# Keys of a cross-attention left unnormalized, and their last tiles shared between batches

## The chip, the core and the metric

The kernel runs on one core of a Trainium2 chip. The core has five engines that work side by side, each through its own instructions in order: TensorE (PE in the profile; its weight loads are PEld), VectorE (DVE), ScalarE (ACT), GpSimd (POOL), and SyncE (SP), which here issues all DMA transfers. Engines wait for each other through semaphores. The metric is device time in microseconds (us) of one execution; lower is better. Time before: median 2002.96 us of three runs (2000.17 to 2003.44).

## What is computed

One block of a Perceiver: x has 8 batches of 64 tokens with 512 features, the context 8 batches of 1601 tokens. A cross- and self-attention block, a sparse self-attention and a feed-forward network are added to x in turn. The part that matters here is the cross attention, with 8 groups of keys (128 features each) and two heads per group:

```python
kvx = jnp.einsum('bsi,oi->bso', cond, w_kv_x)
kx, vx = jnp.split(kvx, 2, axis=-1)
kx = _ln(kx.reshape(b, sc, g, d), kxln_w, kxln_b)
vx = vx.reshape(b, sc, g, d)
xout = _gqa(qx, kx, vx).reshape(b, s, nh * d)
```

`_ln` takes the mean off, multiplies by `rsqrt(var + 1e-5)`, then by a weight and adds a bias, both along the features. `_gqa` is softmax of q k / sqrt(128) over the 1601 tokens, times v.

## The kernel before

The cross attention is done in 16 pieces of work (class `Cross`): two halves of four key groups, and in each half the 8 batches. A batch's 1601 tokens are 13 tiles (`TT`), twelve of 128 tokens and a last one of 65; its tiles form six chunks (`CHUNKS`), five of two tiles and a last one of three, 321 tokens. So there are 208 steps (variable `g` in the main loop at L1142), with one tile of keys each; other work is laid between them.

Per tile, `keys` (L529) loads the transposed context (`cTr`), splits it into a high and a low part (`cThi` by ACT, `cTlo` by POOL), and multiplies both with the key weights, high and low, in 12 matmuls (L542) whose moving side is 512 columns, the four groups' features. [...] `key_weights` (L491) has taken the mean out of the weights, so that keys come out centred. ACT squares (`sq`, L547) and copies (`kn`, L548) the result; DVE sums the squares by group (`kxv`, L549), POOL adds epsilon and raises to -1/2 (`rqk`, L550 and L173), and DVE multiplies the keys by it (L552). One step later `keys_t` (L555) transposes the tile on PE (L219), ACT writes weight times key plus bias as the high part (`kthi`, L565), DVE subtracts it (`kf`, L567), and ACT adds the bias and writes the low part (`ktlo`, L568).

When a chunk is complete, `scores` (L570) multiplies the queries, high and low, with the keys of each group (L587), three matmuls a group, into banks of PSUM. DVE copies each group's scores to SBUF (`S`) while it takes their maximum (`cmx`, L591); the second operand of that instruction is a column of zeros. For the last chunk the odd 321st column is padded to 322 with zeros by POOL (L576, L577). `maxima` (L594) reduces the chunks' maxima, and `exps` (L598) takes the exponentials with the negative maximum as ACT's bias. 16 steps after a tile's keys, `probs_t` (L604) transposes its probabilities, `context` (L636) loads the context, and `weigh` (L661) multiplies them (L676 to L678). `values` and `cat` follow at the end of a batch.

Between the steps the loop pumps streams of other work (projections, self attention, output projections, the conversion of the feed-forward weights) at fixed paces; `pin` and `paced` name an instruction after which the pumped work may be issued. Within each engine the order is set when the program is built, by a scheduler that simulates time; on the chip each engine takes its instructions in that order.

PSUM tiles come from three pools: `pm` (tag m, 3 banks: keys, scores, transposed probabilities), `pb` (one), and `pacc` (4, the sums of `weigh`). `kf` has two buffers of 2 KB per partition, also used by `key_weights` at the start (L495) and by the last attention (`pd`, L155).

Of the kernel before, what the change touches and what calls it, by code (L numbers as in the profile page):

```python
# [11 lines left out]
F32 = mybir.dt.float32  # L12
F32R = mybir.dt.float32r
# [8 lines left out]
P = 128  # L22
# [13 lines left out]
CHUNKS = [(0, 1), (2, 3), (4, 5), (6, 7), (8, 9), (10, 11, 12)]  # L36
KTW = 324
NCH = len(CHUNKS)
CHUNK_OF = {tt: ci for ci, ch in enumerate(CHUNKS) for tt in ch}
LAG = 17  # L40
ALL = 10 ** 6
# [4 lines left out]
PACE = 1.55, 4  # L46
LATER = 142
TERNARY_PACE, TERNARY_AT = 0.4, 8
HELD = "held"


# [6 lines left out]
def tile_perceiver(ctx: ExitStack, tc: tile.TileContext, t: dict):  # L58
# [18 lines left out]
    def nm(s):  # L77
        uid[0] += 1
        return f"{s}_{uid[0]}"
# [62 lines left out]
    class Late:  # L142
# [9 lines left out]
        fb = _main("cThi", 2)  # L152
        ld = _main("qxlo", 1)
        xrt = _main("qxhi", 1)
        pd = _main("kf", 2)  # L155
        ps = staticmethod(lambda tag="b": kxp())

        AT = {"hT": (0, 0), "ps_": (0, 0), "qkv": (0, 256), "sim": (0, 448), "mask": (1, 0), "eq": (1, 64), "cum": (1, 128),
# [332 lines left out]
    def key_weights(half):  # L491
        hi = mp.tile([P, NIC, 512], F32R, tag="wkhi", name=nm("wkhi"), bufs=1)
        lo = mp.tile([P, NIC, 512], F32R, tag="wklo", name=nm("wklo"), bufs=1)
        for ic in range(NIC):
            tag, bufs = ("kf", 2) if half == 0 and ic >= 2 else ("raw", 3)  # L495
            raw = load(mp.tile([P, 512], F32, tag=tag, name=nm("wkr"), bufs=bufs), t["wkv"][ic * P:(ic + 1) * P, half * 512:(half + 1) * 512])
            raw3 = v3(raw, HG)
            mu = sm("wkmu", HG)
            V.tensor_reduce(mu, raw3, AX.X, ALU.add)
            V.scalar_tensor_tensor(raw3, mu.unsqueeze(2).to_broadcast([P, HG, D]), -1.0 / D, raw3, ALU.mult, ALU.add)  # L500
            A.copy(hi[:, ic, :], raw)
            (V if half else GP).tensor_tensor(lo[:, ic, :], raw, hi[:, ic, :].bitcast(F32), ALU.subtract)
        return hi, lo

    paced = [None]
    pin = [None]

    class Cross:


        def __init__(self, b, half):
            self.b, self.half = b, half
            self.raw = None
            self.S = {}
            self.kt = {}
            self.kn = {}
            self.pp = {}
            self.cc = {}
            self.mx = sm("cmx", HG * NCH, bufs=2)
            self.su = sm("csu", HG * NCH, bufs=2)  # L520

# [7 lines left out]
        def keys(self, tt):  # L529

            t0, n = TT[tt]
            raw = mp.tile([P, NIC, P], F32, tag="raw", name=nm("cTr"), bufs=3)
            paced[0] = nc.sync.dma_start(raw[:, :, :n], t["ctxT"][self.b].rearrange("(c p) k -> p c k", p=P)[:, :, t0:t0 + n])
            chi = mp.tile([P, NIC, P], F32R, tag="cThi", name=nm("cThi"), bufs=2)
            clo = mp.tile([P, NIC, P], F32R, tag="cTlo", name=nm("cTlo"), bufs=2)
            A.copy(chi[:, :, :n], raw[:, :, :n])  # L536
            GP.tensor_tensor(clo[:, :, :n], raw[:, :, :n], chi[:, :, :n].bitcast(F32), ALU.subtract)  # L537
            ps = kxp()
            k = 0
            for st, mv in ((chi, self.wk[0]), (chi, self.wk[1]), (clo, self.wk[0])):  # L540
                for ic in range(NIC):
                    PE.matmul(ps[:n], lhsT=st[:, ic, :n], rhs=mv[:, ic, :], start=k == 0, stop=k == 11)  # L542
                    k += 1
            kn = mp.tile([P, 512], F32, tag="kn", name=nm("kn"), bufs=3)
            sq = mp.tile([P, 512], F32, tag="sq", name=nm("sq"), bufs=1)
            v = sm("kxv", HG)
            A.activation(sq[:n], ps[:n], AF.Square, scale=1.0 / math.sqrt(D))  # L547
            A.copy(kn[:n], ps[:n])  # L548
            V.tensor_reduce(v[:n], v3(sq[:n], HG), AX.X, ALU.add)  # L549
            GP.tensor_scalar(v[:n], v[:n], EPS, None, ALU.add)  # L550
            r = rsqrt(v[:n], n, HG, "rqk")
            pin[0] = V.tensor_tensor(v3(kn[:n], HG), v3(kn[:n], HG), r.unsqueeze(2).to_broadcast([n, HG, D]), ALU.mult)  # L552
            self.kn[tt] = kn

        def keys_t(self, tt):  # L555

            t0, n = TT[tt]
            ci = CHUNK_OF[tt]
            c0 = TT[CHUNKS[ci][0]][0]
            if ci not in self.kt:  # L560
                self.kt[ci] = [mp.tile([P, HG, KTW], F32R, tag="kt" + x, name=nm("kt" + x), bufs=2) for x in ("hi", "lo")]
            hi, lo = self.kt[ci]
            pt = transpose4(self.kn.pop(tt), n, kxp())
            o = slice(t0 - c0, t0 - c0 + n)
            A.activation(hi[:, :, o], v3(pt, HG)[:, :, :n], AF.Identity, bias=hb["kx"], scale=hw["kx"])  # L565
            kf = mp.tile([P, HG, P], F32, tag="kf", name=nm("kf"), bufs=2)
            V.scalar_tensor_tensor(kf[:, :, :n], v3(pt, HG)[:, :, :n], hw["kx"], hi[:, :, o].bitcast(F32), ALU.mult, ALU.subtract)  # L567
            A.activation(lo[:, :, o], kf[:, :, :n], AF.Identity, bias=hb["kx"])  # L568

        def scores(self, ci):  # L570
            chunk = CHUNKS[ci]
            cw = sum(TT[tt][1] for tt in chunk)
            hi, lo = self.kt.pop(ci)
            N = cw + (cw & 1)
            if N > cw:
                GP.memset(hi[:, :, cw:N].bitcast(F32), 0.0)  # L576
                GP.memset(lo[:, :, cw:N].bitcast(F32), 0.0)  # L577
            sc = mp.tile([P, HG, KTW], F32, tag="S", name=nm("S"), bufs=7)
            self.S[ci] = sc
            per = 512 // N  # L580
            for g0 in range(0, HG, per):
                bank = mainp("s")
                gs = range(g0, g0 + per)

                for k, (a, x) in enumerate(((self.qhi, hi), (self.qlo, hi), (self.qhi, lo))):
                    for i, g in enumerate(gs):
                        PE.matmul(bank[:, i * N:(i + 1) * N], lhsT=a[:, g * P:(g + 1) * P], rhs=x[:, g, :N],  # L587
                                  start=k == 0 and i == 0, stop=k == 2, skip_group_check=True)
                for i, g in enumerate(gs):
                    ps = bank[:, i * N:(i + 1) * N]  # L590
                    V.tensor_tensor_reduce(sc[:, g, :cw], ps[:, :cw], zeros.to_broadcast([P, cw]), 1.0, -3.0e38,  # L591
                                           ALU.add, ALU.max, self.mx[:, g * NCH + ci:g * NCH + ci + 1])

        def maxima(self):  # L594
            self.nmx = sm("cnm", HG)
            V.tensor_reduce(self.nmx, v3(self.mx, HG), AX.X, ALU.max, negate=True)  # L596

        def exps(self, ci, g0=0, g1=HG):  # L598
            cw = sum(TT[tt][1] for tt in CHUNKS[ci])
# [367 lines left out]
            xs.append((xr, j * P, i * P, P))  # L967
        return z, xs

    def gp_copy(dst, src):  # L970
        GP.tensor_scalar(dst, src, 1.0, 1.0, ALU.mult, ALU.mult)  # L971

    WIDEN = gp_copy, A.copy

    def ffn_weights(f, kind):
# [151 lines left out]
            token_norm(j)  # L1127
            yield

    NT = len(TT)  # L1130
    work = [Cross(b, half) for half in range(2) for b in range(NB)]
    NA = NT * len(work)
    rest = range(1, NJ)
# [8 lines left out]
    for g in range(NA + LAG + 3):  # L1142
# [24 lines left out]
            last_context()  # L1167
        if g < NA:
            work[nA].keys(kA)
        if g == 0:  # L1170
            bgA.pump(ALL)
        if g == 2:
            bgA.add(norms(rest), projection("qx", range(4), rest), projection("qx", range(4, 8), range(NJ)),
                    projection("q", range(8), range(NJ)), projection("k", range(4), range(NJ)), projection("v", range(4), range(NJ)))
# [134 lines left out]
```

## Time and profile before

| | us |
|---|---|
| median of the runs | 2002.96 |
| profiled execution, its own time | 1998.47 |
| span of its instructions | 1996.7 |
| PE busy | 1931.5 (97%) |
| PEld busy | 1594.1 (80%) |
| DVE busy | 1357.9 (68%) |
| ACT busy | 1345.9 (67%) |
| POOL busy | 682.7 (34%) |
| DMA engines, mean busy share | 55.8% |

The profile is of one execution. The span runs from the first to the last instruction; the execution's own time includes 1.8 us around it. In a row of instructions, "busy" is the time in which at least one of the group ran, followed by the mean length of one in nanoseconds, and then the idle time of the engine before them and what ended it. Matmuls overlap each other, so that their lengths add up to more than their busy time. The granted clock of TensorE was 0.987 on average.

### The profile page before, as it was taken

The page shows a single profiled execution, that of the slowest core. Times are in us where ns is not written, and L with a number is a line of the kernel's source. Part 1 is how long each engine was busy: PE and PEld are TensorE (multiplying, and loading weights), DVE is VectorE, ACT ScalarE, POOL GpSimd, SP SyncE. Part 2 cuts the span into 40 slices and gives each one's busy share as a digit, 9 for nine tenths or more (in the row PEclk, how much of TensorE's full clock was granted, in tenths as well). Part 3 has the DMA queues.
Part 4 walks back from the last instruction along what each step waited for, and adds up shares of the span by engine and source line. Part 5 has one row for each costly group of instructions (what it writes and reads, how often), then busy time and mean ns, then how long its engine had stood idle before and what let it go on. Part 6 is the DMA issues. An engine that isn't in the chain of part 4 may idle for free. (4 is left out here: it accounts for less than half of the span.)

```text
span 1996.7 us, 32526 instructions
## 1 busy us (share of the span) xinstructions
PE 1931.5 (97%) x10709; PEld 1594.1 (80%) x10709; DVE 1357.9 (68%) x3324; ACT 1345.9 (67%) x2932; POOL 682.7 (34%) x807
## 2 busy tenths in 40 slices
PE   6899999999999999999999999999999999999998
PEld 5688887888888888888888888888877777886776
DVE  6868678667778677766775765666577665665665
ACT  6777777677778667765765655665786676676554
POOL 5443434333334434323233323323333323320132
PEclk9999999999999999999999999999999999999989
DMA  6354445466455654556886667656744633564415
GB/s 195 112 151 148 148 146 153 132 193 213 152 150 172 194 179 140 173 180 224 282 268 192 214 225 264 203 185 214 258 133 154 212 110 97 165 205 139 149 56 172
DMA packets 296507, 352.05 MB, mean 176 GB/s; under 512 B 30337, under 2 KB 191233, under 8 KB 296337
## 3 DMA queue, kind: packets, MB, share of 16 engines
q1 hardware_dynamic: 296336, 349.97, 55.8%
q8 instruction: 84, 1.38, 0.3%
q14 instruction: 87, 0.70, 0.1%
HBM read 283.94 MB, written 65.68 MB: 175 GB/s over the span
## 5 line engine op out<-in xcount | busy, mean ns | idle before, releaser
L537 POOL TENSOR_TENSOR cTlo<-cTr,cThi 128x512 fp32r<-128x512 f32 (+1 forms) x208 | 271.1, 1303 | 840.7 <-PE kx L542 443.8
L677 PE MATMUL acc<-plo,chi 128*128 128x512 f32 x768 | 311.7, 406 | 1.0 <-DVE plo L624 1.0
L678 PE MATMUL acc<-phi,clo 128*128 128x512 f32 x768 | 303.4, 396 | 0.0
L549 DVE TENSOR_REDUCE kxv<-sq 128x4 f32<-128x512 f32 (+1 forms) x208 | 141.9, 682 | 228.0 <-ACT sq L547 227.7
L542 PE MATMUL kx<-wkhi,cThi 128*128 128x512 f32 (+1 forms) x832 | 244.3, 415 | 6.6 <-DVE cmx L591 2.5
L676 PE MATMUL acc<-phi,chi 128*128 128x512 f32 x768 | 237.8, 403 | 4.6 <-ACT chi L653 3.4
L565 ACT ACTIVATE kthi<-kx,cols 128x512 fp32r<-128x512 f32 (+1 forms) x208 | 159.5, 767 | 106.8 <-PE kx L219 105.1
L542 PE MATMUL kx<-wklo,cThi 128*128 128x512 f32 (+1 forms) x832 | 231.0, 398 | 0.0
L542 PE MATMUL kx<-wkhi,cTlo 128*128 128x512 f32 (+1 forms) x832 | 226.3, 393 | 0.0
L173 POOL TENSOR_TENSOR rqk<-kxv,mhalf 128x4 f32<-128x4 f32 (+1 forms) x208 | 219.9, 1057 | 16.6
L653 ACT CAST chi<-cr 128x512 fp32r<-128x512 f32 x192 | 118.9, 619 | 137.7 <-PE acc L677 126.2
L536 ACT CAST cThi<-cTr 128x512 fp32r<-128x512 f32 (+1 forms) x208 | 125.6, 605 | 120.0 <-PE kx L542 48.4
L601 ACT ACTIVATE S<-S,cnm 128x256 f32<-128x256 f32 (+1 forms) x384 | 196.8, 520 | 1.5 <-DVE cnm L596 1.5
L567 DVE SCALAR_TENSOR_TENSOR kf<-kx,cols,kthi 128x512 f32<-128x512 f32 (+1 forms) x208 | 151.1, 726 | 60.0 <-ACT kthi L565 58.8
L542 PEld LDWEIGHTS kx<-wklo,cThi 128*128 128x128 f32 (+1 forms) x832 | 156.2, 188 | 39.7
L542 PEld LDWEIGHTS kx<-wkhi,cTlo 128*128 128x128 f32 (+1 forms) x832 | 153.5, 185 | 39.3 <-issue 0.8
L552 DVE TENSOR_TENSOR kn<-kn,rqk 128x512 f32<-128x512 f32 (+1 forms) x208 | 144.7, 695 | 57.0 <-POOL rqk L173 55.5
L542 PEld LDWEIGHTS kx<-wkhi,cThi 128*128 128x128 f32 (+1 forms) x832 | 147.2, 189 | 40.8 <-DVE cmx L591 5.0
L591 DVE CUSTOM_DVE_ANT_0 S<-s,zeros 128x256 f32<-128x256 f32 (+1 forms) x384 | 149.7, 429 | 43.8 <-PE s L587 43.5
L568 ACT ACTIVATE ktlo<-kf,cols 128x512 fp32r<-128x512 f32 (+1 forms) x208 | 147.4, 709 | 29.0 <-DVE kf L567 28.5
L676 PEld LDWEIGHTS acc<-phi,chi 128*128 128x128 f32 x768 | 139.0, 189 | 34.9 <-ACT chi L653 4.6
L677 PEld LDWEIGHTS acc<-plo,chi 128*128 128x128 f32 x768 | 145.2, 189 | 25.7 <-DVE plo L624 1.5
(339 smaller groups left out, 3938.3 us busy)
## 6 DMA issues: line engine op xcount, KB each, us to landing
cTr<-in_ctxT SPq DMA_DIRECT2D x192, 256.0 KB
cr<-in_ctx SPq DMA_DIRECT2D x192, 256.0 KB
ws<-wpd SPq DMA_DIRECT2D x88, 512.0 KB
clod<-clo SPq DMA_DIRECT2D x96, 256.0 KB
clo<-clod SPq DMA_DIRECT2D x96, 256.0 KB
wv<-in_wkv SPq DMA_DIRECT2D x64, 256.0 KB
tern<-in_ffn_w SPq DMA_DIRECT2D x64, 256.0 KB
wpd<-ws SPq DMA_DIRECT2D x32, 512.0 KB
```

The costliest lines, as they stand in the source:

```text
L173: GP.tensor_tensor(y[:n], v, mhalf[:n, :k], ALU.pow)
L537: GP.tensor_tensor(clo[:, :, :n], raw[:, :, :n], chi[:, :, :n].bitcast(F32), ALU.subtract)
L542: PE.matmul(ps[:n], lhsT=st[:, ic, :n], rhs=mv[:, ic, :], start=k == 0, stop=k == 11)
L552: pin[0] = V.tensor_tensor(v3(kn[:n], HG), v3(kn[:n], HG), r.unsqueeze(2).to_broadcast([n, HG, D]), ALU.mult)
L565: A.activation(hi[:, :, o], v3(pt, HG)[:, :, :n], AF.Identity, bias=hb["kx"], scale=hw["kx"])
L567: V.scalar_tensor_tensor(kf[:, :, :n], v3(pt, HG)[:, :, :n], hw["kx"], hi[:, :, o].bitcast(F32), ALU.mult, ALU.subtract)
L568: A.activation(lo[:, :, o], kf[:, :, :n], AF.Identity, bias=hb["kx"])
L591: V.tensor_tensor_reduce(sc[:, g, :cw], ps[:, :cw], zeros.to_broadcast([P, cw]), 1.0, -3.0e38, ALU.add, ALU.max, self.mx[:, g * NCH + ci:g ...
L601: A.activation(self.S[ci][:, g, :cw], self.S[ci][:, g, :cw], AF.Exp, bias=self.nmx[:, g:g + 1], accum_out=self.su[:, g * NCH + ci:g * NCH ...
L676: PE.matmul(self.U[ic], lhsT=chi[:n, s], rhs=phi[:n], start=tt == 0, stop=False)
L677: PE.matmul(self.U[ic], lhsT=chi[:n, s], rhs=plo[:n], start=False, stop=False)
L678: PE.matmul(self.U[ic], lhsT=clo[:n, s], rhs=phi[:n], start=False, stop=False)
```

## The change

Four things change. First, keys are no longer multiplied by their norm, and the bias is left off: `turned` writes weight times raw key as high part (ACT) and low part (DVE). The norms `rqk` go to a buffer in DRAM (`rd`), and when a chunk's last tile is done, `spread` loads the chunk's norms back into all 128 partitions (`rb`, tokens by groups). The evictions of the scores multiply by `rb` where they read zeros before. The product of query and bias is the same for all tokens and falls out of the softmax; it is computed as one more column of keys, in place of the padding column of the last chunk, and copied out (`cqb`), and `maxima` adds it and takes it off again.

Second, the last 64 full tokens of two neighbouring batches share one tile of keys of 128, computed in the step of the even batch; the odd batch has no key matmuls in its last step. Batches 0 and 1 of the first half keep a last tile of 65 each. Third, the 1601st tokens of all 8 batches form one small tile per half (`odd_keys`, at steps 30 and 110), whose keys are stored beside the bias column and copied into place by ACT. Fourth, the scratch for software DMAs is declared smaller; `rb` takes the place of `kf` wherever that served.

```diff
+    def raw_keys(wk, chi, clo, n, held=False):
+        ps = kxp()
+        k = 0
+        for st, mv in ((chi, wk[0]), (chi, wk[1]), (clo, wk[0])):
+            for ic in range(NIC):
+                PE.matmul(ps[:n], lhsT=st[:, ic, :n], rhs=mv[:, ic, :], start=k == 0, stop=k == 11)
+                k += 1
+        kn = mp.tile([P, 512], F32, tag="kn2" if held else "kn", name=nm("kn"), bufs=1 if held else 3)
...
+        pin[0] = V.tensor_reduce(v[:n], v3(sq[:n], HG), AX.X, ALU.add)
+        GP.tensor_scalar(v[:n], v[:n], EPS, None, ALU.add)
+        r = rsqrt(v[:n], n, HG, "rqk")
+        return kn, r
+
+    def turned(kn, n, parts, r0=0):
+        hi, lo = parts
+        pt = kxp()
+        for g in range(HG):
+            PE.transpose(pt[:, g * P:g * P + n], kn[:, g * P:(g + 1) * P], ident[r0:r0 + n, r0:r0 + n])
+        src = v3(pt, HG)[:, :, :n]
+        A.activation(hi, src, AF.Copy, scale=hw["kx"])
+        V.scalar_tensor_tensor(lo, src, hw["kx"], hi.bitcast(F32), ALU.mult, ALU.subtract)
+
+    def odd_keys(half):
+        raw = load(mp.tile([P, 512], F32, tag="raw", name=nm("oc"), bufs=3)[:NB], t["ctx"][:, SC - 1, :])
+        pt = kxp()
+        for ic in range(NIC):
+            PE.transpose(pt[:, ic * NB:(ic + 1) * NB], raw[:, ic * P:(ic + 1) * P], ident[:NB, :NB])
...
+        kn, r = raw_keys(wk[half], chi, clo, NB)
+        oddr[half] = dtile([NB, HG], F32, f"oddr{half}")
+        nc.sync.dma_start(oddr[half], r)
...
+        turned(kn[:NB], NB, [x[:, :, :, 0] for x in oddk[half]])
...
         def keys(self, tt):
             t0, n = TT[tt]
+            pair = tt == NT - 1 and self.paired
+            if pair and self.b % 2:
+                return
...
-            A.activation(sq[:n], ps[:n], AF.Square, scale=1.0 / math.sqrt(D))
-            A.copy(kn[:n], ps[:n])
-            V.tensor_reduce(v[:n], v3(sq[:n], HG), AX.X, ALU.add)
-            GP.tensor_scalar(v[:n], v[:n], EPS, None, ALU.add)
-            r = rsqrt(v[:n], n, HG, "rqk")
-            pin[0] = V.tensor_tensor(v3(kn[:n], HG), v3(kn[:n], HG), r.unsqueeze(2).to_broadcast([n, HG, D]), ALU.mult)
+            kn, r = raw_keys(self.wk, chi, clo, n, pair)
             self.kn[tt] = kn
+            if pair:
+                nxt = work[self.half * NB + self.b + 1]
+                nxt.kn[tt] = kn
+                self.rt = nxt.rt = dram.tile([P, HG], F32, tag="rt", name=nm("rt"), bufs=2)
+                nc.sync.dma_start(self.rt, r)
+                return
...
+            nc.sync.dma_start(self.rd[ci][o:o + n], r)
+
+        def spread(self, ci):
+            cw = sum(TT[tt][1] for tt in CHUNKS[ci])
+            rb = self.rb[ci] = mp.tile([P, KTW, HG], F32, tag="rb", name=nm("rb"), bufs=RB)
...
+            for o, src in parts:
+                w = src.shape[0]
+                load(rb[:, o:o + w].rearrange("p t g -> p (t g)"), src.rearrange("t g -> (t g)").partition_broadcast(P))
...
-            A.activation(hi[:, :, o], v3(pt, HG)[:, :, :n], AF.Identity, bias=hb["kx"], scale=hw["kx"])
-            kf = mp.tile([P, HG, P], F32, tag="kf", name=nm("kf"), bufs=2)
-            V.scalar_tensor_tensor(kf[:, :, :n], v3(pt, HG)[:, :, :n], hw["kx"], hi[:, :, o].bitcast(F32), ALU.mult, ALU.subtract)
-            A.activation(lo[:, :, o], kf[:, :, :n], AF.Identity, bias=hb["kx"])
+            r = self.b % 2 * S
+            turned(kn[r:r + S], S, [x[:, :, o:o + S] for x in self.kt[ci]], r)
+            for x, y in zip(self.kt[ci], oddk[self.half]):
+                A.copy(x[:, :, o + S:o + S + 2], y[:, :, self.b, :])
...
-                    V.tensor_tensor_reduce(sc[:, g, :cw], ps[:, :cw], zeros.to_broadcast([P, cw]), 1.0, -3.0e38,
-                                           ALU.add, ALU.max, self.mx[:, g * NCH + ci:g * NCH + ci + 1])
+                    V.tensor_tensor_reduce(sc[:, g, :cw], ps[:, :cw], rb[:, :cw, g], 1.0, -3.0e38,
+                                           ALU.mult, ALU.max, self.mx[:, g * NCH + ci:g * NCH + ci + 1])
+                    if N > cw:
+                        V.tensor_copy(self.qb[:, g:g + 1], ps[:, cw:N])
 
         def maxima(self):
+            top = sm("ctop", HG)
+            V.tensor_reduce(top, v3(self.mx, HG), AX.X, ALU.max)
+            V.tensor_tensor(top, top, self.qb, ALU.add)
             self.nmx = sm("cnm", HG)
-            V.tensor_reduce(self.nmx, v3(self.mx, HG), AX.X, ALU.max, negate=True)
+            V.tensor_tensor(self.nmx, self.qb, top, ALU.subtract)
...
         if g < NA:
             work[nA].keys(kA)
+            if kA == CHUNKS[CHUNK_OF[kA]][-1]:
+                work[nA].spread(CHUNK_OF[kA])
...
+        if g in ODD_AT:
+            odd_keys(work[nA].half)
...
-    nc = _bacc.Bacc("TRN2", target_bir_lowering=False, num_devices=1)
+    nc = _bacc.Bacc("TRN2", target_bir_lowering=False, num_devices=1, dynamic_dma_scratch_size=1024)
```

Constants: `UNPAIRED = 2`, `ODD_AT = 30, 110`, `RB = 2` (buffers of `rb`, 5 KB per partition each). `self.paired` is true for all batches of the second half and for batches 2 to 7 of the first.

## The prediction

> **What bounds the kernel.** I read the page's totals first, then the stretches, then single instructions of TensorE. Columns of the first two rows: the share of each engine; of the stretches: length, then busy time and count of PE, PEld, DVE, ACT, POOL, the granted clock, DMA share, GB/s.
>
> ```profile
> span 1996.7 us, 32526 instructions
> PE 1931.5 (97%) x10709; PEld 1594.1 (80%) x10709; DVE 1357.9 (68%) x3324; ACT 1345.9 (67%) x2932; POOL 682.7 (34%) x807
> ...
> 0.00:100.00 100.00, 75.82 (x382) 61.57 (x383) 76.31 (x215) 71.43 (x149) 51.82 (x67) 0.94 0.51 154
> ...
> 1000.00:1400.00 400.00, 397.62 (x2203) 334.71 (x2202) 252.47 (x560) 244.33 (x525) 128.67 (x153) 1.00 0.68 222
> ...
> 1800.00:1996.70 196.70, 180.73 (x998) 133.59 (x994) 120.37 (x283) 106.64 (x206) 43.78 (x49) 0.94 0.43 130
> ```
>
> PE is full except in the first 100 us and, less, the last 200; no other engine passes 77% in any stretch. [...] So I look at starts, not at busy time (timeline of PE; start, length, instruction):
>
> ```profile
> 1782.81 1.10 PE L542 MATMUL kx<-wklo,cThi 128*65 128x512 f32 x4
> 1783.75 1.10 PE L542 MATMUL kx<-wkhi,cTlo 128*65 128x512 f32 x4
> 1784.69 0.60 PE L219 MATMUL kx<-ident,kn 128*128 128x128 f32 x4
> ...
> 1791.78 0.41 PE L219 MATMUL kx<-ident,kn 65*128 65x65 f32 x4
> 1792.03 0.60 PE L613 MATMUL pt<-ident,S 128*128 128x128 f32 x4
> ```
>
> Four matmuls of 512 columns start 0.94 us apart from the next four: one occupies PE for **0.235 us**, not the 0.4 us of its row, and the 65-row tile pays as much as a full one. Over the whole trace, start-to-start steps longer than is usual for the same pair of instructions add up to 143 us, some 83 of them between 200 and 1800 us. So PE is occupied about 93% of the span: nearer to the 97% than to the 80%. A PE instruction removed is time removed, at 0.235 us.
>
> **Part 1, tiles of keys (PE).** Before, 16 tiles of 65 tokens pay 12 matmuls each. After, batches 0 and 1 of the first half keep theirs (2), the other 14 share 7, and the odd tokens take 2 tiles: 11. The built order shows 2496 key matmuls becoming 2436. 60 x 0.235 = **14.1 us off**. Transposes: 64 of 65 columns become 8 of 65, 56 of 64, and 16 of 8 for the odd tokens; by the fence four small ones take 0.25 us, so 16 more cost **1.0 us**. Scores, probabilities and contexts keep every PE instruction. PE: **-13.1 us**, nearly all in the stretch that is full.
>
> **Part 2, the norm leaves the keys (DVE, ACT).**
>
> ```profile
> L552 DVE TENSOR_TENSOR kn<-kn,rqk 128x512 f32<-128x512 f32 x192 | 133.7, 696 | 51.0 <-POOL rqk L173 49.7
> ...
> L568 ACT ACTIVATE ktlo<-kf,cols 128x512 fp32r<-128x512 f32 x192 | 139.1, 724 | 26.9 <-DVE kf L567 26.6
> ...
> L885 DVE TENSOR_TENSOR ps__4142_16875<-pr x1: 357/357/357, 1548.6 to 1548.6; 128x192 f32<-128x192 f32 x1
> ...
> L888 DVE TENSOR_TENSOR ps__4142_16875<-ps__4142_16875,pmx x1: 347/347/347, 1550.7 to 1550.7; 128x192 f32<-128x192 f32 x1
> ...
> L897 DVE TENSOR_REDUCE ao<-pr x4: 811/836/855, 1555.8 to 1957.8; 128x64 f32<-128x384 f32 x3, 64x64 f32<-64x384 f32 x1
> ```
>
> All 208 multiplies by the norm go (page: 208 x 695 ns = 145 us of DVE), and all 208 second ACT passes over the low part (208 x 709 ns = 147 us). The low part is written by the DVE instruction that wrote kf (L567), so its count stays but for the tiles; five fewer reduces (L549) give 3.4 us.
>
> What comes in return is the read in the eviction of the scores (L591, 384 of them): it multiplies by rb[:, :, g], whose elements stand 16 bytes apart, where before it read one constant. The trace has no row of exactly this. [...] The rows agree in kind: 8-byte steps (L885) cost as much as contiguous ones (L888), 256-byte steps (L897) 836 ns for 384 elements and (L887) 505 for 192, so 1.72 ns an element, where the evictions themselves go from 418 ns at 256 to 486 at 321, or 1.05. Ends: 0 if the step is free, +0.68 ns an element if it costs what L897 pays. [...] With 64 copies of one column (164 ns by L817) and two more small operations per batch, 16 us: DVE 1358 - 145 - 3 + 70 + 16 = 1296 us (1226 at the other end); ACT 1346 - 147 - 6 for fewer tiles + 28 copies x 0.2 (L633) = 1199. POOL loses 32 memsets and five tiles' small operations, about 10 us. The two odd tiles bring some ten small operations each to these engines, about 1 us apiece. The smaller scratch for software DMAs costs nothing: the page's DMA queues show hardware ones alone.
>
> None of this is on PE's path in the full stretches; priced at 0 there, PE hides it. At the start PE waits 5.3 us in all for L552 before key transposes (who-waits view of L219); these waits end with ACT's copy kn instead: **-2 us**. Against it, PE waits 11.5 us for score evictions (L591), which hold banks that keys need too; a chunk's four evictions get 0.7 us longer while DVE has two multiplies, 1.4 us, less to do per chunk: between -2 and +10, taken at **+1**.
>
> **Part 3, the relay of the norms (SP, DMA).** Each tile now stores 128 x 4 values, and 96 chunks load them back to all partitions. The built order has 1368 SP DMAs becoming 1697: 203 stores of 2 KB, 124 loads (94 of 512 KB, 2 of 642 KB for the unpaired last chunks, 28 small pieces) and 2 loads of odd tokens. At 0.32 to 0.42 us of SP each (clod and cTr at 708.12 and 705.48 us in the timeline) that is 115 us more of SP's time, on 623. The bytes: 52 MB on 352, so the DMA share goes from 56% to about 64%, and from 68% to about 77% at 1000 to 1400 us.
>
> Two waits are new on SP, which issues in order: the store waits for rqk, the load for the store's landing. Behind them stand the next ctxT and ctx loads and the stores of clo. SP waits already:
>
> ```profile
> SPq L533 <- POOL kxv L550: 223.0, 91, 6.4
> SPq L130 <- PE acc L678: 158.1, 78, 5.3
> SPq L658 <- DVE clo L657: 144.5, 58, 7.6
> ```
>
> They are waits for free buffers; the loads land 2.4 us (median) before ACT's copy, and ACT's cThi is ready 13.4 us before its first matmul (7.0 at the lowest twentieth), chi 11.6 before its own. A hold of SP of some 2 us per chunk is within this; without the cover it would be 96 x 2 = 190 us, and 0 is the other end. I take **+1**.
>
> The relay itself: store 1.6 us (simd, 4 KB) to 2.3 (clod, 256 KB) from issue to landing, then the load like ws from wpd, also 512 KB: 4.8 median, 3.6 to 6.9 between the tenths. Together with SP's 0.4: 5.6 to 9.6 us, typically 7.5. It has from the end of a chunk's last rqk to its first eviction: in the trace 16.0 us median, 12.3 at the lowest tenth, 8.4 at least, and in the built order the evictions stand equally many key tiles behind. So it fits nearly always; a few chunks at the start and at the ends of batches may hold DVE's queue (kxv, plo behind it), **+1**. With two rb buffers a load waits for the evictions two chunks back, some 40 us earlier. The shared tile's kn2, one buffer, is held 13 tiles and wanted again after 26: no wait.
>
> **Sum.** -13.1 - 2 + 1 + 1 + 1 = **-12 us**. The profiled execution took 1998.5 us (span 1996.7): 1986.5. The median of the runs is 2003.0, 4.5 above it, so I forecast **1991 us**; 0.2% (4 us) is about what can be told from no change.
>
> **Rivals.**
> - *Forecast*, PE's saving passes through: 1984 to 1998; 0.52.
> - *More than PE's own*: ACT and DVE lose 150 and 60 us, so part of the 83 us of steps that are too long in the middle goes too; a quarter of it gives 20 more: 1971. For it: ACT's and DVE's queues feed phi, plo and chi. Against: the named PE waits are few, each under 5 us. 0.16.
> - *Cancelled*: more DMA load and SP holds cost 10 to 14 us, spread: about 2002; 0.14.
> - *The relay decides (slower)*: one mechanism, rb late at the evictions in DVE's in-order queue. It decides once the relay exceeds about 12 us, where a tenth of the chunks lack time; at 16 us half of them wait about 2 us each, 96 us of DVE holds, and if a third reaches PE it is +32 - 12: 2023. For it: SP's order adds holds in front of the store; against: 4 us of spare at the median even then. 0.18.
> - That fewer matmuls are not there is excluded by the built order.
>
> Faster 0.70, same 0.12, slower 0.18. The range leaves out the far end of the relay and of the larger gain: 1974 to 2012; the likeliest one's own is 1984 to 1998.
>
> **What would show it.** Right: L542's line with 2436 matmuls and PE busy down by about 12 us; evictions at 590 ns for 256 columns; DVE near 1296, ACT near 1199; rb landing before the eviction; PE's idle time unchanged. Wrong: a wait of S for rb among the longest of DVE, PE waiting for cmx by tens of us, or cThi and chi waiting for their loads.

## The result, and the profile after

The changed kernel takes **2089.7 us** (median of 4 runs, 2086.4 to 2094.3), the kernel before 2003.2 beside it: a ratio of 1.0437, 95% interval 1.0415 to 1.0459. The forecast was 1991. The profiled execution took 2094.3 us with a span of 2092.1, where the one before had 1998.5 and 1996.7: 95 us more.

The same rows as before, from the page of the changed kernel and its stretches (first the shares of the span; then length, busy time and count of PE, PEld, DVE, ACT and POOL, granted clock, DMA share, GB/s):

```profile
span 2092.1 us, 32927 instructions
PE 1959.3 (94%) x10665; PEld 1599.2 (76%) x10665; DVE 1311.9 (63%) x3214; ACT 1202.5 (57%) x2739; POOL 680.4 (33%) x766
...
DMA packets 343239, 404.95 MB, mean 194 GB/s; under 512 B 62972, under 2 KB 225660, under 8 KB 343068
...
L611 ACT CAST cThi<-cTr 128x512 fp32r<-128x512 f32 (+1 forms) x201 | 124.7, 620 | 300.0 <-DMA cTr<-in_ctxT 187.1
...
L680 DVE CUSTOM_DVE_ANT_0 S<-s,rb 128x256 f32<-128x256 f32 (+1 forms) x384 | 225.5, 625 | 37.0 <-PE s L676 32.9
```

```profile
0.00:100.00 100.00, 70.48 (x332) 58.16 (x333) 64.28 (x180) 53.70 (x115) 47.68 (x63) 0.88 0.55 165
1000.00:1400.00 400.00, 382.04 (x2063) 314.15 (x2062) 233.14 (x509) 204.94 (x468) 121.83 (x136) 1.00 0.75 235
```

The sums of the forecast for the other engines came true: DVE 1312 (1296 forecast), ACT 1202.5 (1199), and there are 60 key matmuls fewer. And yet PE, which was to be busy 12 us less, is busy 28 us more and idle too. In the stretch from 1000 to 1400 it was busy 397.6 of 400 us before, now 382.0, with 2063 matmuls done in place of 2203. No engine became the bound in its place: all are less busy there than before. This is the picture of an engine that is fed late, everywhere a little.

PE's own waits confirm it. Added up by the engine that ended them, they are 49.8 us for ACT (21.7 before), 53.1 for DVE (28.6) and 21.6 for loads (6.5). Some rows, before and then after (total us, times, longest):

```profile
PE pp L431 <- DMA ws<-wpd: 2.5, 3, 1.3
PE kx L542 <- ACT kn L548: 1.2, 2, 0.8
PE acc L676 <- ACT phi L623: 1.1, 3, 0.5
```

```profile
PE pp L435 <- DMA ws<-wpd: 17.0, 15, 3.6
PE acc L771 <- ACT phi L718: 8.6, 7, 2.7
PE kx L544 <- ACT kn L533: 6.5, 6, 2.3
```

Where the lateness comes from is told by the longest waits of SP's queue and of ACT in the changed kernel, with one row of ACT before behind them:

```profile
SPq L134 <- DMA rd<-rqk: 154.8, 82, 5.8
SPq L626 <- POOL rqk L177: 134.5, 120, 5.8
SPq L608 <- POOL kxv L535: 130.0, 68, 4.5
...
ACT cThi L611 <- DMA cTr<-in_ctxT: 187.1, 67, 7.8
ACT chi L748 <- PE acc L772: 100.4, 62, 5.6
```

```profile
ACT cThi L536 <- DMA cTr<-in_ctxT: 16.0, 16, 3.0
```

SP now waits 155 us for stores of norms to land and 135 us for the norms themselves. These waits largely stand in place of waits for free buffers that it had anyway: all of SP's waits together are 1353 us, before 1431. So their length does not tell what they cost. ACT waits 187 us for tiles of ctxT to arrive, where it waited 16 before. ACT works in order and runs nothing in these 67 waits: behind a cThi that waits stand kn, sq, phi and kthi, and PE's waits for kn and phi have grown as shown. The norms on their way through DRAM, however, are in time: DVE waits only 3.8 us for rb in all, and rb lands 9.0 us (median) before the chunk's first eviction. The slower rival of the prediction, rb late at the evictions, is not what happened.

The clock is a smaller part. TensorE ran at half speed for 89 us in all, 55 before. If half of such a stretch is lost, that is some 17 of the 95 us (an estimate). In the first 100 us, where PE is least busy, the granted clock is 0.88, before 0.94. I count the clock with the waits; no run here tries one without the other.

### The profile page after: what moved, and what is told of

Same layout as the page of the kernel before. It is cut to its first block, busy times and chain, and to the rows that moved or that the text cites. A ratio compares the mean times of both kernels' runs of the same rounds, so it can differ in the third digit from the quotient of the medians.

```text
span 2092.1 us, 32927 instructions
## 1 busy us (share of the span) xinstructions
PE 1959.3 (94%) x10665; PEld 1599.2 (76%) x10665; DVE 1311.9 (63%) x3214; ACT 1202.5 (57%) x2739; POOL 680.4 (33%) x766
## 5 line engine op out<-in xcount | busy, mean ns | idle before, releaser
L527 PE MATMUL kx<-wkhi,cThi 128*128 128x512 f32 x812 | 237.9, 414 | 19.5 <-DVE cmx L680 5.9
L680 DVE CUSTOM_DVE_ANT_0 S<-s,rb 128x256 f32<-128x256 f32 (+1 forms) x384 | 225.5, 625 | 37.0 <-PE s L676 32.9
L527 PE MATMUL kx<-wklo,cThi 128*128 128x512 f32 x812 | 229.8, 403 | 0.0
L527 PE MATMUL kx<-wkhi,cTlo 128*128 128x512 f32 x812 | 226.9, 398 | 0.0
L547 DVE SCALAR_TENSOR_TENSOR ktlo<-kx,cols,kthi 128x512 fp32r<-128x512 f32 (+2 forms) x208 | 150.7, 725 | 94.2 <-ACT kthi L546 92.8
L546 ACT ACTIVATE kthi<-kx,cols 128x512 fp32r<-128x512 f32 (+2 forms) x208 | 140.5, 676 | 93.7 <-PE kx L544 92.8
L527 PEld LDWEIGHTS kx<-wkhi,cThi 128*128 128x128 f32 x812 | 145.3, 191 | 57.3 <-DVE cmx L680 9.3
L527 PEld LDWEIGHTS kx<-wklo,cThi 128*128 128x128 f32 x812 | 154.5, 191 | 39.0 <-issue 1.6
L527 PEld LDWEIGHTS kx<-wkhi,cTlo 128*128 128x128 f32 x812 | 152.9, 189 | 39.2 <-issue 2.4
L771 PEld LDWEIGHTS acc<-phi,chi 128*128 128x128 f32 x768 | 140.9, 191 | 41.7 <-ACT phi L718 11.6
L773 PEld LDWEIGHTS acc<-phi,clo 128*128 128x128 f32 x768 | 145.5, 190 | 25.3 <-issue 0.8
```

What stands on the lines that cost most here:

```text
L546: A.activation(hi, src, AF.Copy, scale=hw["kx"])
L547: V.scalar_tensor_tensor(lo, src, hw["kx"], hi.bitcast(F32), ALU.mult, ALU.subtract)
L680: V.tensor_tensor_reduce(sc[:, g, :cw], ps[:, :cw], rb[:, :cw, g], 1.0, -3.0e38, ALU.mult, ALU.max, self.mx[:, g * NCH + ci:g * NCH + ci + 1])
L771: PE.matmul(self.U[ic], lhsT=chi[:n, s], rhs=phi[:n], start=tt == 0, stop=False)
L773: PE.matmul(self.U[ic], lhsT=clo[:n, s], rhs=phi[:n], start=False, stop=False)
```

## The experiments

All times are medians of whole runs, ratios are against the kernel before on the same chip (1998 to 2000 us there). One thing must be kept in mind when reading them: the build lays out each engine's order anew for each kernel from its own estimate of times, so two variants seldom have PE's instructions in the same order. Differences of some us between neighbours may come from that, and one case below shows 13 us. One pair, told below, has the same order on every engine. The clock also differs: the time lost to it (one less the granted share, times the span; medians of each kernel's runs) is 18 to 20 us for the kernel before and 42 for the changed one.

**Taking the change apart: four variants.** The shared tiles alone, with norm and bias still on the keys and no relay (in `raw_keys` the multiply stays, in `turned` the bias and kf):

```diff
+        pin[0] = V.tensor_tensor(v3(kn[:n], HG), v3(kn[:n], HG), r.unsqueeze(2).to_broadcast([n, HG, D]), ALU.mult)
...
-            work[nA].spread(CHUNK_OF[kA])
```

> Only the sharing of the last tiles: 11 last tiles of keys instead of 16, norm and bias stay on the keys, no relay, evictions read zeros. If the part of the sum for TensorE was right (60 matmuls of 0.235 us less, 16 small transposes more) and the loss comes from the norm's new place, this takes 13 us off: 1986 to 1994 us. If the sharing itself does harm (odd batches with a step without key matmuls, a tile held for 13 steps), it is above 2003.

It took **2019.0** (ratio 1.0102, 1.0081 to 1.0123). The part that was to bring 13 us costs 19.

The norm on the scores alone, with the relay, all last tiles unshared:

```diff
-ODD_AT = 30, 110
+ODD_AT = ()
...
-            self.paired = half > 0 or b >= UNPAIRED
+            self.paired = False
```

> Only the move of norm and bias to the scores: 16 last tiles of 65 as before, no small tile of odd tokens, relay of the norms through DRAM for every chunk. If the loss comes from this part, 2095 to 2110 us (the changed kernel plus the 13 us that it saved); if it came from the sharing, about 2005.

**2058.6** (1.0293, 1.0273 to 1.0314): 59 us over the kernel before, the larger part of the loss. With the 19 of the shared tiles that makes 78 of the 87 to 90.

The whole change without the relay: no store, no load of norms; the evictions read a constant tile of the same shape and step, so the scores are not normalized:

```diff
+    rbc = ctile([P, KTW, HG], F32, "rbc")
+    V.memset(rbc, 0.05)
...
-            nc.sync.dma_start(self.rd[ci][o:o + n], r)
...
-            rb = self.rb.pop(ci)
+            rb = rbc
```

> The changed kernel without the relay: no stores of the norms, no loads of rb; the evictions read a constant buffer with the same 16-byte step (so the scores are not normalized). All DVE and ACT work stays. If the relay (SP's waits or its traffic) is the cause: 1983 to 1995 us, with ACT's wait for cTr back near 16 us. If the slower evictions on DVE are the cause: still above 2050.

**2010.5** (1.0053, 1.0033 to 1.0073). So the relay costs 79 us, and what is left without it still isn't faster.

The relay's loads alone (124, 52 MB), from a buffer in DRAM that is written once at the start, without the stores; the scores are multiplied by ones, so not normalized:

```diff
-            parts = [(0, self.rd.pop(ci)[:cw])]
+            parts = [(0, rdc[:cw])]
...
-            nc.sync.dma_start(self.rd[ci][o:o + n], r)
```

> The changed kernel with the 124 loads of rb, all of their 52 MB, but from a DRAM buffer written once at the start: no stores of norms and no wait for a store's landing (the scores are multiplied by ones). If SP's new waits are the cause: 1985 to 2005 us. If the traffic of the loads is the cause: 2060 to 2090. If both share it, about 2040.

**2035.3** (1.0177, 1.0157 to 1.0197): 25 us for loads that wait for nothing.

**What is it in the relay?** The stores alone (the stores of the changed kernel put back into the variant without relay, whose constant tile the evictions read):

> The changed kernel with the 203 small stores of the norms kept and every load of them left out: the evictions read a constant tile at the same 16-byte step, so the scores are not normalized. Theory A (SP is held twice per chunk, by the store that waits for rqk and by the load that waits for the store to land; of the changed kernel's 59 us over the run with loads alone, the two waits share in the ratio of their traced length, 134 to 155 us): 2010 + about 27 = 2030 to 2045. Theory B (only the load's wait for the landing counts, the rqk wait is short each time): within 6 us of the kernel without relay, 2005 to 2017. Theory C (the stores' 26000 packets of 16 bytes slow the other transfers): over 2045, with the landing of ctxT loads at 3.5 us or more.

**2051.0** (1.0249, 1.0185 to 1.0312): the number of Theory C, 40 us for 0.4 MB. Then each store cut to one packet, with its SP instruction and its wait kept:

```diff
-            nc.sync.dma_start(self.rd[ci][o:o + n], r)
+            nc.sync.dma_start(self.rd[ci][o:o + 1], r[:1])
```

> The run with stores alone, with each store cut to the norms of one token: 16 bytes in one packet, where it was 128 packets. The SP instructions and their waits for rqk stay (the run with stores alone took 2051, the one without relay 2010); the scores are not normalized. Theory A (the 26000 packets of 16 bytes slow the other transfers): 2012 to 2022, cTr's loads back to 3.1 to 3.2 us from issue to landing. Theory B (SP's issues and its waits for rqk make the loads late): 2040 to 2052, landing shorter but ACT's wait for cTr still near 90 us.

**2027.1** (1.0131, 1.0088 to 1.0174), between the two theories. Some 17 us come with SP's 203 instructions and their waits for rqk (167 us of SP; ACT's wait for cTr is 67 us, 56 without stores), and 24 us with 28,400 small packets: 25,400 of the stores' 16 bytes and 3,000 of 4 bytes, of which each whole store has 16 and each cut one has one. With two runs of each of these two kernels the 24 is uncertain by some 15 us either way and the 17 by some 9, and the order of the instructions differs too, so that both parts are there but their sizes are rough. The pages, stores alone first, then one packet:

```profile
DMA packets 325382, 352.47 MB, mean 172 GB/s; under 512 B 59196, under 2 KB 220092, under 8 KB 325212
```

```profile
DMA packets 296944, 352.05 MB, mean 174 GB/s; under 512 B 30758, under 2 KB 191654, under 8 KB 296774
```

The bytes are equal to 0.1%. The loads of ctx take 3.70 us from issue to landing with the packets and 2.95 without, those of ctxT 3.55 and 3.23 (medians over the trace; 2.96 and 3.04 before, 4.32 and 3.88 in the changed kernel). Next, the complete change with its stores and loads issued by POOL, which makes rqk itself, the load a step later:

```diff
-            nc.sync.dma_start(self.rd[ci][o:o + n], r)
+            GP.dma_start(self.rd[ci][o:o + n], r)
```

> The changed kernel, complete, with the stores and loads of the norms issued by POOL instead of SP, the load a step later: POOL makes rqk itself, so SP waits for neither rqk nor a landing, while the traffic stays. Theory A (SP's holds make ctxT and context loads late, and these reach PE over ACT's queue): SP's waits for rqk go, ACT's 187 us of waiting for cTr falls to the 115 us of the run with loads alone, and the time to 2025 to 2045. Theory B (traffic and the relay's small packets decide): 2075 to 2100. Theory C (POOL, held by the landing, takes SP's place: cTlo and rqk late): over 2100, with PE waiting for cTlo.

**2076.8** (1.0376, 1.0336 to 1.0415). SP's two new waits are gone, ACT still waits 139 us for cTr, and 13 of 90 us come back. POOL takes a part of SP's place (it waits 144 us for landings), but the transfers are as slow as with SP: 3.93 us for ctxT, 4.19 for ctx. This speaks against SP's holds as the greater part and for the late loads, but as POOL is held instead, it does not settle it.

**Is it late loads, then?** The next run keeps relay and traffic. It gives the loads of ctxT and ctx one buffer more, so that they can be issued a tile earlier:

```diff
-            raw = mp.tile([P, NIC, P], F32, tag="raw", name=nm("cTr"), bufs=3)
+            raw = mp.tile([P, NIC, P], F32, tag="raw", name=nm("cTr"), bufs=4)
```

> The changed kernel, complete, with one more buffer for the loads of ctxT and ctx (4 in place of 3), so that they can be issued a tile earlier; relay, SP's waits and traffic stay. Theory A (the loads come too late for ACT's in-order queue, because their cushion of 2.2 us was smaller than the relay's delay): ACT's wait for cTr falls from 187 us to under 60, and the time to 2020 to 2050. Theory B (DMA traffic or PE's order by itself): within 10 us of the changed kernel, 2080 to 2095.

**2040.0** (1.0196, 1.0156 to 1.0236): 50 of the 87 us come back. Its longest waits of ACT and of SP's queue:

```profile
ACT chi L748 <- PE acc L772: 148.4, 77, 6.5
ACT kthi L546 <- PE kx L544: 110.5, 75, 6.2
ACT cThi L611 <- PE kx L527: 77.5, 48, 7.4
...
ACT cThi L611 <- DMA cTr<-in_ctxT: 22.3, 13, 3.4
```

```profile
SPq L626 <- POOL rqk L177: 146.5, 121, 5.2
SPq L134 <- DMA rd<-rqk: 145.7, 84, 4.2
```

SP waits as long as in the changed kernel, and its loads of ctxT are even slower (4.79 us), but ACT waits 22 us for them and not 187. They land 4.0 us before ACT's copy (median), in the changed kernel 0.84, before 2.24. PE's waits for ACT fall to 30.2 us with them (for kn from 13.4 to 2.1, for phi from 8.8 to 3.0). So the same waits of SP now reach ACT and PE much less. PE's own wait for ws is still 11.6 us; why those loads are late was not tried.

**Why don't the shared tiles pay?** First without the odd tokens' tiles: their keys are zeros and the last key of every batch is left out.

```diff
-        raw = load(mp.tile([P, 512], F32, tag="raw", name=nm("oc"), bufs=3)[:NB], t["ctx"][:, SC - 1, :])
...
-        turned(kn[:NB], NB, [x[:, :, :, 0] for x in oddk[half]])
+        for x in oddk[half]:
+            GP.memset(x.bitcast(F32), 0.0)
```

> The kernel with the shared tiles alone (norm and bias on the keys, no relay), but without the two tiles of odd tokens: no load, transposes, matmuls or norm for them, their keys are zeros, so the last key of every batch is left out. Theory A (the two odd tiles, whose chain of load, transposes, copy, matmuls, copy, transposes stands in PE's order, cost some 12 us each, pauses and the half-speed clock behind them): 2019 - 25 = about 1990 to 1996, faster than before. Theory B (they cost what their matmuls take, 24 x 0.235 = 6 us and some transposes; the rest of the loss is in the uneven steps of the pairs): 2008 to 2014. Theory C (any new order of the instructions costs about this): no closer than 2012.

**1995.2** (0.9975, 0.9963 to 0.9988), 24 us less: Theory A. Two tiles of 8 rows cost as much as a hundred key matmuls at 0.235 us. Where, is seen in PE's timeline of the shared tiles alone, at the second of the two (start, length, instruction, idle time before it):

```profile
967.24 1.07 PE L522 MATMUL kx<-wkhi,cTlo 128*8 128x512 f32 x4
970.41 0.66 PE L223 MATMUL tr<-ident,fa 128*128 128x128 f32 x4 [2.10 <-DVE fa L477]
972.07 2.07 PE L489 MATMUL po<-fb,ld 64*128 64x128 f32 x8 [1.01 <-ACT fb L481]
...
979.07 2.06 PE L522 MATMUL kx<-wkhi,cThi 128*128 128x512 f32 x4
```

Behind the odd tile's matmuls PE stands 2.1 us for DVE and then 1.0 for ACT. Both have just had the odd tile's links in their queues; that these made them late is how I read it. After that the clock is halved for 10 us (971.4 to 981.6): four matmuls that take 1.07 us in the first row take 2.06 in the last. Against the kernel before, this variant loses 14 to 16 us between 950 and 980 us and 9 between 240 and 252, where the first odd tile stands. Now the whole work, spread over steps: the odd tokens' context is turned and split once, at the start, the matmuls follow, and the transposes come two steps later.

```diff
-ODD_AT = 30, 110
+ODD_AT = 7, 106
...
+        if g == ODD_AT[0] - 2:
+            odd_context()
         if g in ODD_AT:
             odd_keys(work[nA].half)
+        if g - 2 in ODD_AT:
+            odd_turned(work[nA].half)
```

> The kernel with the shared tiles alone, complete, with the odd tokens' work spread over steps: their context is turned and split once, in step 5 where PE has pauses anyway, and kept; the matmuls stand in steps 7 and 106, and the transposes of their keys two steps later, so that PE never has two links of the chain in a row. Theory A (the chain in PE's order is the cost): 1993 to 2003, at least 15 us below the 2019 of the shared tiles. Theory B (the uneven steps of the pairs cost): 2012 to 2020. If the place matters but the chain does not, between the two.

**2000.5** (1.0001, 0.9985 to 1.0018): 18.5 us gained for nearly the same work (the odd context is turned once, not twice), as Theory A said. Place and splitting were changed together, so their shares are not told apart. Part of the gain is the clock's: the time lost to it is 29 us with the tiles in one piece and 18 here (medians of the runs). But it is level with the kernel before, not 13 us ahead.

**Does the forecast hold without relay and chain?** The change without relay (scores not normalized) and with the odd work so spread:

> The changed kernel without relay (constant tile in the evictions, no stores, no loads; scores not normalized), with the odd tokens' work spread over steps as in the run that brought the shared tiles from 2019 to 2000. It is what the forecast priced, without the relay. Theory A (the losses add: chain of odd tiles 19 us, relay 80): 2010 - 18 = 1990 to 1995. Theory B (the freed time of DVE and ACT also shortens the middle): 1975 to 1988. Theory C (the chain hid another loss): 1998 to 2010.

**2012.0** (1.0062, 1.004 to 1.0085), no gain on 2010.5, just over the range of Theory C. The starts of the same transposes pt in the two traces show why the sum is zero: each odd tile in one piece costs some 6.5 us here too (at 249 and 974 us), but the spread variant loses 13 us between 320 and 605 us, where none of the odd work stands. A new order of the instructions can do that; it was not pursued. So spreading did not help this kernel, and its 18.5 us above hold for that kernel alone.

Something else costs here, and the evictions are what this kernel has and the shared tiles alone do not. The pair with the order unchanged tests it: the constant tile is laid out so that an eviction reads 4-byte steps; nothing else differs (again not normalized).

```diff
-    rbc = ctile([P, KTW, HG], F32, "rbc")
+    rbc = ctile([P, HG, KTW], F32, "rbc")
...
-                    V.tensor_tensor_reduce(sc[:, g, :cw], ps[:, :cw], rb[:, :cw, g], 1.0, -3.0e38,
+                    V.tensor_tensor_reduce(sc[:, g, :cw], ps[:, :cw], rb[:, g, :cw], 1.0, -3.0e38,
```

> The run without relay and with the odd tokens staged (2012), with the constant tile laid out so that an eviction reads 4-byte steps in place of 16-byte ones; nothing else, every engine's instructions stand in the same order. Scores not normalized. Theory A (the longer evictions, 606 ns where it was 429, hold the PSUM banks and DVE's queue, and this is what the norm on the scores costs apart from the relay): 1996 to 2003, no slower than the 2000.5 of the shared tiles with the norm on the keys. Theory B (the evictions are hidden; the order of the instructions or the copies of the bias column cost it): 2008 to 2014.

**1992.0** (0.996, 0.9937 to 0.9982): 20 us, Theory A, a little beyond its better end. The evictions with the 16-byte step, then with the 4-byte one:

```profile
L684 DVE CUSTOM_DVE_ANT_0 S<-s,rbc 128x256 f32<-128x256 f32 x320 | 179.9, 604 | 23.7 <-PE s L680 23.1
L684 DVE CUSTOM_DVE_ANT_0 S<-s,rbc 128x321 f32<-128x321 f32 x64 | 46.3, 725 | 21.8 <-PE s L680 21.8
```

```profile
L684 DVE CUSTOM_DVE_ANT_0 S<-s,rbc 128x256 f32<-128x256 f32 x320 | 120.7, 418 | 27.9 <-PE s L680 27.1
L684 DVE CUSTOM_DVE_ANT_0 S<-s,rbc 128x321 f32<-128x321 f32 x64 | 31.0, 485 | 27.4 <-PE s L680 27.1
```

75 us more of an engine that is busy 63 to 66% make the span 19.5 us longer. As the two traces have the same PE instructions in the same order, the steps from start to start can be subtracted one by one: 8.0 us of it appear in front of or within the key matmuls with cThi and 7.1 at the transposes pt, which take PSUM banks after the scores. One place, PE's and DVE's timelines, slow evictions first:

```profile
754.22 0.60 PE L712 MATMUL pt<-ident,S 128*128 128x128 f32 x4
755.25 1.21 PE L529 MATMUL kx<-wkhi,cThi 128*128 128x512 f32 x4 [0.43 <-DVE cmx L684]
...
754.02 0.64 DVE L684 CUSTOM_DVE_ANT_0 S<-s,rbc 128x256 f32<-128x256 f32 x1
754.58 0.60 DVE L684 CUSTOM_DVE_ANT_0 S<-s,rbc 128x256 f32<-128x256 f32 x1
```

```profile
744.21 0.60 PE L712 MATMUL pt<-ident,S 128*128 128x128 f32 x4
744.57 1.17 PE L529 MATMUL kx<-wkhi,cThi 128*128 128x512 f32 x4
...
743.60 0.41 DVE L684 CUSTOM_DVE_ANT_0 S<-s,rbc 128x256 f32<-128x256 f32 x1
743.94 0.41 DVE L684 CUSTOM_DVE_ANT_0 S<-s,rbc 128x256 f32<-128x256 f32 x1
```

With the short evictions the key matmuls start 0.36 us after pt; with the long ones they wait for the evictions and start 1.03 us after it. Of the whole difference some 8 us stand at PE steps whose wait ended with the evictions' results (cmx, ctop, cqb), 1.5 of them at one place where a subtraction of DVE was slow as well. Some 4 us stand where the clock was halved in one of the two runs: behind a wait of 2.21 us four key matmuls take 2.07 us, in the other run 1.20 behind a wait of 1.51. The rest is scattered over waits for ACT, for other results of DVE and for loads. As nothing but the eviction's step was changed, it follows from that, but link by link it was not traced. PE's busy share of both runs reads 96 to 97%.

**A version that beats both, and its control.** Shared tiles, norm and bias on the keys, odd work spread, all batches paired, four buffers for the loads:

```diff
-UNPAIRED = 2
+UNPAIRED = 0
...
-            raw = mp.tile([P, NIC, P], F32, tag="raw", name=nm("cTr"), bufs=3)
+            raw = mp.tile([P, NIC, P], F32, tag="raw", name=nm("cTr"), bufs=4)
```

> Candidate to beat both: shared tiles with the norm and the bias on the keys (no relay), the odd tokens' work spread over steps, all 16 batches paired (the first two too, 12 matmuls fewer), and 4 buffers for the loads of ctxT and ctx. The version with 3 buffers and two unpaired batches took 2000.5. Theory A (late loads cost the kernel before something too): 12 x 0.235 = 3 us and some of ACT's 16 us of waits for cTr: 1985 to 1996, faster than before. Theory B (they are hidden there): 1996 to 2001, no difference that can be told.

**1986.6** (0.9927, 0.9905 to 0.9948), 12 us faster than before. How much of it are the buffers, with nothing else of the change?

> The kernel before, with 4 buffers in place of 3 for the loads of ctxT and ctx (and the smaller scratch of the change, which makes the room). Theory A (the shared tiles have their part in the 1987 of the version with shared tiles and 4 buffers: 15 us of TensorE saved): 1994 to 2002, little or no gain. Theory B (the buffers alone make it): 1984 to 1991.

**1996.6** (0.9981, 0.9969 to 0.9993), 3.4 us. The other 10 come with the shared tiles, but only together with the buffer and the pairing of all batches: with three buffers and two batches unpaired these tiles gained nothing (2000.5). Of the 10, some 6 are the clock's (12 us lost to it here, 18 with the buffers alone, medians of the runs). Last, the complete change mended in the same three ways:

> The whole change, complete, with what the other runs pointed to: odd tokens staged, all batches paired, 4 buffers for ctxT and ctx. With 4 buffers alone it took 2040. Theory A (the odd chain costs its 19 us here too): 2015 to 2025. Theory B (as without relay, where staging gave nothing: 2010.5 and 2012): 2033 to 2042. Either way over the 1987 of the shared tiles without moved norm.

**2051.8** (1.0265, 1.0228 to 1.0302), 12 us more than with the fourth buffer alone: a miss for both theories. ACT waits 43 us for cTr here, 22 there, so in places the loads are late again; why was not pursued. With the relay in it, the change stays slower in every form that was run.

## Why the prediction was wrong

The likeliest case had -12 us. Something near it came out for one kernel only, the one without relay, with short evictions and with the odd work spread: 1992.0, 8 us under the kernel before. Even that is in part luck, since the shared tiles from which the gain was to come brought nothing by themselves (2000.5). From there to the 2089.7 of the change: the 16-byte step +20 (to 2012.0), the odd work in one piece 0 within that kernel (2010.5, the net of two things as told above), the stores +40 and the loads +25 each taken alone, and 14 more for both together with the wait for the landing.

- *"Part 1 ... PE: -13.1 us"*: the number of matmuls was right. With each PE instruction counted at its median step to the next start, over both traces, the spread variant's sum is 12 us shorter than before (1878.5 after 1890.5; 6 us if pairs of neighbours are counted). What failed is that it passes through. "The two odd tiles bring some ten small operations each to these engines, about 1 us apiece" priced work, not order: as one chain the two cost 18.5 us more than spread. And even spread, what is left of the span beside that sum grew by 11 us (106 to 117). The transposes pt alone take 12 us more (94.9 after 83.0); three of their steps last 2.2 to 2.5 us, where none before was over 0.9. Why is open. "A PE instruction removed is time removed" was the author's estimate, from PE being occupied about 93% of the span; in this kernel 60 key matmuls fewer gained no time (2000.5). A small term was missed too: four 64-row transposes take PE 0.39 us from start to start where four 65-row ones took 0.245, 2 us for the 14 groups.
- *"None of this is on PE's path in the full stretches; priced at 0 there, PE hides it"*, with "taken at **+1**" for the evictions. The size of the step was right: 0.73 ns an element of 256 (604 and 418 ns), forecast 0.68. The +70 in the forecast's sum for DVE was an estimate from one row of another instruction (L897); no run shows that term, and in its place the pair with the order unchanged showed 75 us. Where the step would cost was wrong: an eviction holds a bank that PE wants, and 75 us of DVE came to PE as **20 us**. The forecast had a range of -2 to +10 for it, from 11.5 us of waits that PE was said to show; the rows of the kernel before give 6.4 for its matmuls (pt 3.9, kx 2.5) and 13.9 for its weight loads. Either way these were the waits for evictions of 418 ns, and longer evictions made new ones where PE had not waited.
- *"A hold of SP of some 2 us per chunk is within this ... I take +1."* This is the step that failed most. The cushion was read at its median, 2.4 us from a load's landing to ACT's copy. Its lower quarter was 1.14 us and its lower tenth 0.17: there was none where it counts. In the changed kernel the median itself is 0.84 us, and ACT waits 187 us in place of 16. The 13.4 us from cThi to its matmul did not help, since ACT works in order: a cThi that waits also holds kn, sq and phi, and PE now waits 13.4 us for kn and 8.8 for phi. The fourth buffer brings 50 us back. The same buffer brings 3.4 us in the kernel before, and 14 with the shared tiles and all batches paired. So some 36 to 46 of the relay's 79 us, about half, arise at these late loads; the other half is not traced further.
- *"The bytes: 52 MB on 352, so the DMA share goes from 56% to about 64%"*: true (64.0%), and priced at nothing. The relay's loads alone, with their traffic and SP's 124 more instructions, cost 25 us. The stores were priced by their 2 KB; their small packets cost some 24 us (uncertain by some 15). The runs show the cost, not what makes it.
- *"5.6 to 9.6 us, typically 7.5 ... So it fits nearly always"*: right. The stores land in 2.9 us, the loads in 4.7 (medians), rb comes 9.0 us early, and DVE waits for it 3.8 us in all.
- *The rivals*: "The relay decides" had the right part and the wrong place: it decides by what it does to other transfers, not by arriving late. "Cancelled" named the right mechanism, "more DMA load and SP holds", at 10 to 14 us, a sixth of its size. "More than PE's own" did not show in the changed kernel, with some 140 us less of ACT and 46 less of DVE. It is not excluded: without relay and with short evictions, the kernel that frees ACT and DVE takes 1992.0 where the shared tiles alone take 2000.5. The order of the instructions differs in this pair, so the cause of the 8 us is open.

## What to carry to other kernels

Read a cushion at its lower tenth, not at its median (0.17 and 2.4 us here), and before adding transfers ask which in-order queue stands behind the load that will come late: one more buffer there brought 50 us back here, where the change was to bring 12. DVE at 63 to 66% was not free here, where its instruction held a bank that the bound engine wanted next: 75 us of longer evictions came to the span as 20; price the longer eviction on the path. A short new chain that goes through the full engine several times is priced by its links in that engine's order; laid out over several steps it was 18.5 us cheaper in one kernel here, and no cheaper in another whose order changed against it.

## What the runs showed of the hardware

- Small packets: with 203 stores of 2 KB (0.4 MB; 28,400 packets more, of 16 and 4 bytes) the ctx loads take 3.70 us from issue to landing, where they take 2.95 with one packet a store. In the run with the 124 loads of 52 MB, without stores, it was 3.59; in the kernel before, 2.96.
- An eviction of the scores that reads its constant tile in 16-byte steps took DVE 604 ns where one with 4-byte steps took 418, for 256 elements of f32 on 128 partitions; at 321 elements 725 and 485 (the pair with the order unchanged).
- Four transposes of 64 rows in a row took PE 0.112, 0.062, 0.063 and 0.152 us from start to next start, almost the same in each of the 14 groups of the shared tiles (one group had a pause behind the last). Four of 65 rows before took 0.060 to 0.063 each, but for two groups of 16. So the 64-row ones cost 0.145 us more a group, at its first and its last step. What makes it was not tried.
